# Hybrid attention and mixing layers: sums of products by twos in PSUM, word joins on GpSimd, shifted rows in PSUM, and a new order

## The chip, the cores and the metric

The kernel runs on one core of one Trainium2 chip. Its time is the device time of one execution in microseconds. Before the change three runs gave 1161.39, 1161.8 and 1164.65 us, median 1161.8. The engines are named as the profile names them: PE is TensorE (PEld its weight loads), DVE is VectorE, ACT is ScalarE, POOL is GpSimd, SP is SyncE, which here only issues DMAs.

## The reference

The input x has 8 sequences of 512 rows with 256 channels, all float32. Four layers follow each other; each takes the layer norm of x and adds its result to x:

```python
x = x + attn_a(layernorm(x))   # Q, K l2-normed; Q * mean over rows of K * V
x = x + ffn(layernorm(x))
x = x + attn_b(layernorm(x))   # 16 heads of 64, softmax over the queries
x = x + ffn(layernorm(x))      # the same weights as above

def ffn(x):                    # x_prev is x shifted down by one row, row 0 zero
    xr = mu_r * x + (1 - mu_r) * x_prev
    xk = mu_k * x + (1 - mu_k) * x_prev
    r = sigmoid(xr @ W_r.T)
    return r * (square(relu(xk @ W_k.T)) @ W_v.T)
```

In `attn_b` the projections q, k and v of one sequence are products of its 512 x 256 rows with 256 x 1024 weights, plus a bias each; the softmax runs over axis 2, the queries of the scores.

## The kernel before

The sequences b = 0 to 7 are worked on in halves h of 256 rows. A front of a sequence is `attn_a`, the first `ffn` and the norm of `attn_b`; then come 8 pairs of heads (g counts pairs over all sequences, 0 to 63); a tail is the second `ffn` with the write of the result.

**Attention.** `attend` (L1037) takes two pairs of heads at once: for each chunk c of 128 keys it issues the scores (`scores`, L959, four 64x512 matmuls into a pair of PSUM banks, a maximum on VectorE at L976), the context of the pair before (`context`, L1011) and the exponentials (`exps`, L981, ScalarE). `scale_v` (L995) divides the values by the sums: a reciprocal on VectorE (L1000) and a product on GpSimd (L1004), which the contexts wait for.

**Between two attention blocks** the other work is placed. Each piece is a Python generator, a chain, that yields before each step the engine, an assumed duration and when its input is ready; `Order` (L75) is a planner that runs in Python while the program is built. It keeps a clock for each engine, adds what a result takes to reach another engine (`PASS`, L33), and picks the chain whose next step can start first, with due times, and a rank that can be shifted by a pseudo-random number (`turn`, L171) seeded per block from the table `CHOICES`. What comes out is one fixed order of instructions; every engine works through its own part of it in order. PSUM is five slots for this: three pairs of banks, shared with the scores, and two single banks, shared with the contexts. A step on TensorE takes a slot (`take`, L107) and the chain gives it back (`give`, L128).

**Products.** For q, k and v of sequences 1 to 7, and of sequence 0 behind its first pairs and values, a 2 x 2 product of blocks is made with seven block products instead of eight (`seven`, L752), from sums of weights (`sums_of_weights`, L703, once) and of rows (`sums_of_rows`, L717, once for each sequence). A block product is `mul` (L813 for q and k, L848 for v): two 128x256 matmuls, each on its own half of a bank. There are 31 such chains for q and k (`project_pairs`, L803, two pairs of heads each) and 14 for v (`values_fast`, L841). The products are joined in SBUF: each goes into a bank of its own, which is read and given back, in the order 1, 6, 2, 7, 5, 4, 3. Product 1 is copied with its bias (`begin`: L823 on ScalarE for q and k, L860 on VectorE for v), products 6, 2, 4 and 3 are added by VectorE (L770, L774, L788, L792), product 7 with the difference of the biases (`join`: L831 for q and k; L867 and a GpSimd add at L870 for v), product 5 is copied by ScalarE (L780) and added twice by GpSimd (L783, L785).

**Norm and transposition.** `normed` (L349) takes mean and variance on VectorE (L355, L356), the sign change of the mean on VectorE (L372), the root and the shift on GpSimd (L374 to L376), and the scaling on ScalarE (L379); with `early` set the scaling is VectorE's (L365) and there is no shift. The transposed rows come either from TensorE (`normed_t`, L385, four 128x128 transposes for each half) or from a DMA transpose, which works on 16-bit words (`normed_dma`, L398): GpSimd splits the low and high words into two planes (L405, two copies), SyncE issues the transpose (L410), ScalarE joins the words (L414, one copy of 128x1024 words). The DMA way is taken for all norms of sequences 2 to 7 in the fronts and for the tails but the last.

**Mixing.** In `ffn` (L443) ScalarE writes the rows scaled by 1 - mu into two buffers, one row further on (L465), saves the last row of the first half (L462) as the edge of the second, VectorE fills the edge (L472) and adds mu times the rows (L479, two operations for each of xk and xr). Then TensorE makes k (L491), r and o (both in `rows`, L426), ScalarE takes the relu, the square and the tanh (L498, L501, L505), VectorE multiplies (L510) and `add_to` (L514) adds to x.

**Names.** Buffers come in two sets, with False and True in their names: xn, xp, xr, xk. The set True belongs to sequence 1's front and then to the tails of sequences 0 to 6. In the DMA way xr holds the split words, xk the transposed ones; xr (for mixing) or xp or xta (for products) holds the joined rows. `tr_*` are PSUM tiles of transposes, `m_qk` and `m_v` those of block products, sc scores, cx contexts.

## Time and profile before

| what | value |
|---|---|
| median of three runs | 1161.8 us (1161.39 to 1164.65) |
| the profiled execution, its own time | 1162.71 us |
| its span, from the first to the last instruction | 1160.8 us |
| mean granted clock of TensorE | 0.994 |
| instructions | 19186 |
| busy: PE, DVE, ACT, POOL | 97%, 69%, 63%, 42% of the span |
| DMA | 29.17 MB, mean 25 GB/s |

The profile is of one execution. A group row of it names line, engine, operation, the tiles written and read, partitions x elements and the count; behind the first bar stand the busy time in us and the mean ns of one instruction, behind the second the idle time of the engine just before them and what ended it. A row of the view of waits reads: engine, tile and line that waited, what it waited for, then the total in us, how many times, and the longest. A row of the timeline starts with the start and the length in us; in square brackets stands the idle time before it. In the view by windows each engine's busy time stands with its number of instructions, then the granted clock of TensorE, the DMA share and GB/s. Instructions of one engine overlap a little, so that a matmul's recorded length is longer than the distance to the next: two matmuls of 128x256 (four records) are 0.86 us apart from the next two.

### The profile page before, as it was taken

The numbers are of one execution on the slowest core, as the hardware profiler recorded it, in microseconds if no ns is written. First come the engines' busy times: TensorE is split into PE (matmuls) and PEld (weight loads), VectorE is DVE, ScalarE is ACT, GpSimd is POOL, SyncE is SP. The second block draws the span as 40 slices with busy tenths as digits, with TensorE's granted clock in tenths as the row PEclk, the third lists the DMA queues.
The fourth block names the chain that finished last, engine by engine and source line by source line (L and its number), as shares of the span: only waits on it lengthen the run. The fifth ranks groups of instructions, "written<-read, shape, count | busy, mean of one in ns | idle before, by whom it ended". The sixth has DMA issues, their size and how long they took to land.

```text
span 1160.8 us, 19186 instructions
## 1 busy us (share of the span) xinstructions
PE 1129.8 (97%) x7012; PEld 703.9 (61%) x7012; DVE 806.4 (69%) x1384; ACT 730.6 (63%) x1802; POOL 485.7 (42%) x702
## 2 busy tenths in 40 slices
PE   6999899999999999999999999999999999999997
PEld 3646466655668566656666655766657655666556
DVE  5676776777866767776886667676776777656853
ACT  3666575677855767657585568456774776556643
POOL 5465434443337334345532444442546343433211
PEclk9999899999999999999999999999999999999999
DMA  8000000110102100012000120001110100000001
GB/s 294 1 1 19 1 19 2 28 20 9 19 1 64 37 1 19 1 46 38 10 10 10 46 38 1 10 19 37 24 32 15 24 11 10 19 10 11 10 1 37
DMA packets 63294, 29.17 MB, mean 25 GB/s; under 512 B 53568, under 2 KB 61760, under 8 KB 62688
## 3 DMA queue, kind: packets, MB, share of 16 engines
q1 hardware_dynamic: 62048, 26.22, 9.4%
q8 instruction: 56, 0.92, 0.3%
q10 hardware_dynamic: 864, 1.05, 0.3%
q0 software_dynamic: 288, 0.67, 0.2%
q14 instruction: 38, 0.31, 0.1%
HBM read 10.63 MB, written 4.19 MB: 13 GB/s over the span
## 4 chain that ended last, share of the span: by engine, by line
PE 46%; DVE 2%; issue 1%; ACT 1%; DVEq 0%
PE cx L1024 10%; PE sc L971 10%; PE m_qk L815 8%; PE y L426 5%; PE m_v L850 4%; PE r_g L426 2%; PE o_g L426 2%; PE k_g L491 1%; PE r_f L426 1%; PE kv L571 1%; PE o_f L426 1%; PE k_f L491 1%; PE q L426 1%; DVE xrFalse L479 1%; DVE xrTrue L479 0%
## 5 line engine op out<-in xcount | busy, mean ns | idle before, releaser
L987 ACT ACTIVATE e<-sc,nm 128x512 f32<-128x512 f32 x512 | 346.6, 690 | 126.7 <-DVE nm L976 125.5
L976 DVE TENSOR_REDUCE nm<-sc 128x2 f32<-128x1024 f32 x256 | 307.9, 1216 | 60.9 <-PE sc L971 60.5
L971 PE MATMUL sc<-qk 64*64 64x512 f32 x2048 | 270.5, 600 | 9.4 <-DVE qk L792 8.3
L1024 PE MATMUL cx<-e,vs 64*64 64x512 f32 x2048 | 268.2, 594 | 0.2 <-POOL vs L1004 0.2
L1004 POOL TENSOR_TENSOR vs<-v,rs 128x256 f32<-128x256 f32 x128 | 78.5, 614 | 383.2 <-DVE rs L1000 363.3
L1024 PEld LDWEIGHTS cx<-e,vs 64*64 64x64 f32 x2048 | 85.4, 134 | 139.9 <-issue 115.9
L971 PEld LDWEIGHTS sc<-qk 64*64 64x64 f32 x2048 | 73.8, 133 | 151.4 <-issue 82.7
L426 PE MATMUL y<-al,ctx 128*128 128x256 f32 x512 | 116.3, 380 | 0.0
L426 PEld LDWEIGHTS y<-al,ctx 128*128 128x128 f32 x512 | 96.8, 190 | 17.3 <-ACT e L987 3.2
L987 ACT ACTIVATION_READ_ACCUMULATOR e<-sc,nm 128x1 f32 x512 | 105.6, 206 | 0.0
L1032 DVE TENSOR_TENSOR ctx<-cx,ctx 128x512 f32<-128x512 f32 x64 | 44.2, 691 | 48.0 <-ACT ctx L1031 46.9
L571 PE MATMUL kv<-wkv,xpFalse 128*128 128x512 f32 x112 | 52.4, 607 | 1.1 <-ACT xpFalse L414 1.1
L783 POOL TENSOR_TENSOR qk<-qk,qk 128x512 f32<-128x512 f32 x31 | 40.8, 1315 | 27.8 <-ACT qk L780 26.2
L913 DVE TENSOR_TENSOR x<-y,x 128x512 f32<-128x512 f32 x32 | 22.1, 689 | 39.9 <-PE y L426 39.7
L405 POOL COPY xrFalse<-xnFalse 128x512 uint16<-128x512 uint16 x72 | 42.6, 626 | 8.1 <-ACT xnFalse L379 8.1
L1031 ACT COPY ctx<-cx 128x512 f32<-128x512 f32 x64 | 37.5, 585 | 12.3 <-PE cx L1024 12.3
L517 POOL TENSOR_TENSOR x<-x,xkFalse 128x512 f32<-128x512 f32 x24 | 31.0, 1293 | 29.5 <-DVE xkFalse L510 21.9
L785 POOL TENSOR_TENSOR qk<-qk 128x512 f32<-128x512 f32 x31 | 40.6, 1310 | 2.4
L815 PE MATMUL m_qk<-xts,aq 128*128 128x256 f32 x124 | 37.1, 381 | 3.9 <-DVE v L788 3.9
L815 PE MATMUL m_qk<-xta,aq 128*128 128x256 f32 x124 | 38.2, 390 | 0.0
L770 DVE TENSOR_TENSOR qk<-m_qk,qk 128x512 f32<-128x512 f32 x31 | 21.4, 691 | 23.9 <-PE m_qk L815 23.3
L815 PE MATMUL m_qk<-xta,sums_q 128*128 128x256 f32 x124 | 36.9, 379 | 0.0
(248 smaller groups left out, 2037.5 us busy)
## 6 DMA issues: line engine op xcount, KB each, us to landing
out<-x SPq DMA_DIRECT2D x16, 256.0 KB, 2.1
x<-in_x SPq DMA_DIRECT2D x6, 512.0 KB, 4.3
aq<-in_aq SPq DMA_DIRECT2D x1, 1024.0 KB, 7.9
ak<-in_ak SPq DMA_DIRECT2D x1, 1024.0 KB, 9.9
av<-in_av SPq DMA_DIRECT2D x1, 1024.0 KB, 11.9
al<-in_al SPq DMA_DIRECT2D x1, 1024.0 KB, 14.3
xkFalse<-xrFalse SPq DMA_TRANSPOSE x36, 3.1
x<-in_x SPq DMA_DIRECT2D x4, 128.0 KB, 4.3
```

What stands on the lines that cost most here:

```text
L405: nc.gpsimd.tensor_copy(apart.rearrange("p (l k u d) -> p l k u d", l=2, k=KC, u=2)[:, :, :, u, :], s["xn"].bitcast(U16)[:, h, u, 2:].rear ...
L426: nc.tensor.matmul(ps[:, u * D : (u + 1) * D], lhsT=lhs[i][:, u * P : (u + 1) * P], rhs=rhs[i], start=(i == 0), stop=(i == n - 1),)
L571: nc.tensor.matmul(ps, lhsT=xt[:, kc, u * P : (u + 1) * P], rhs=wkv[:, kc, :], start=(kc == 0), stop=(kc == KC - 1),)
L783: nc.gpsimd.tensor_tensor(c12, c12, c22, ALU.add)
L815: nc.tensor.matmul(ps[:, w * HS : (w + 1) * HS], lhsT=lhs[w][n - 1], rhs=block_of_rows(b, n), start=True, stop=True,)
L850: nc.tensor.matmul(ps[:, u * HS : (u + 1) * HS], lhsT=block_of_rows(b, n)[:, u * P : (u + 1) * P], rhs=rhs[n - 1], start=True, stop=True,)
L971: nc.tensor.matmul(ps[m * HD : (m + 1) * HD, j, :], lhsT=kt[hs, keys], rhs=qt[hs, :], start=True, stop=True,)
L976: nc.vector.tensor_reduce(nm, ps, AX.X, ALU.max, negate=True)
L987: nc.scalar.activation(e[:, j, :], ps[:, j, :], AF.Exp, bias=nm[:, j : j + 1], accum_out=sums[g, h][:, c % 2, j : j + 1],)
L1004: nc.gpsimd.tensor_tensor(vs, vh[b, p // 4][:, 2 * h : 2 * h + 2, cols].rearrange("p t (j d) -> p t j d", j=2), rs.unsqueeze(3).to_broadca ...
L1024: nc.tensor.matmul(cx[m][j * HD : (j + 1) * HD, :], lhsT=vsc[g, c // 2][ks, c % 2, j, :], rhs=es[g, c][ks, j, :], start=(c == 0), stop=(c ...
L1032: nc.vector.tensor_tensor(ct, cx[1], ct, ALU.add)
```

## The change

The seven products are summed by twos in PSUM. Products 1, 6, 7 and 5 take a slot as before, but product 2 is accumulated on the bank of product 1 after that has been read, product 4 on that of 7, and product 3 on that of 5. So the banks of 1, 7 and 5 are held until their second reading, and product 5 is no longer copied and added by GpSimd. For v the difference of the biases is added by GpSimd to the summand before the join. The order of a chain is now 1, 6, 7, 2, 5, 4, 3.

The join of the words behind a DMA transpose moves from ScalarE to GpSimd, and so does the sign change of the mean from VectorE. In the mixing behind a DMA transpose (`mixed_dma`, new) ScalarE writes the shifted rows into a PSUM slot, one for xk and one for xr; VectorE clears the first column there, or fills it with the edge, and adds mu times the rows. The mixing behind TensorE's transposes (`mixed_t`) is what `ffn` did; the first mixings of sequences 0 and 1 take the `early` norm. The first norm of sequence 2 is transposed by TensorE. The planner gets marks that it lacked (the sums of weights, and the use of the buffers by the tail before), gates that open after an attention block, other assumed durations, a smaller allowance for other work inside a block, and a new `CHOICES` table, so that the whole order is a new one. The arithmetic and its types are the same otherwise.

The diff, cut to its core:

```diff
-PASS = {"T": 0.27, "A": 0.2, "V": 0.17, "G": 0.17, "S": 2.0}
+PASS = {"T": 0.27, "A": 0.2, "V": 0.17, "G": 0.17, "S": 2.2}
...
+        self.takes = step[5] if len(step) > 5 else self.on == "T"
...
-    def give(self):
-        self.banks = [self.ended if c is self.current else c for c in self.banks]
+    def give(self, i=None):
+        self.banks = [
+            self.ended if c is self.current and i in (None, n) else c
+            for n, c in enumerate(self.banks)
+        ]
     def ready(self, c):
         ready = max(c.ready, self.marks[c.mark])
-        if c.on == "T":
+        if c.takes:
             slots = self.slots(self.now)
             if slots:
                 ready = max(ready, slots[0][0])
...
         return [
             c for c in self.chains
-            if c.mark in self.marks and c.gate <= self.period
-            and (c.on != "T" or c.cost <= most and self.slots(self.now))
+            if c.mark in self.marks and c.gate <= self.open
+            and (c.on != "T" or c.cost <= most) and (not c.takes or self.slots(self.now))
         ]
...
         else:
             shift = small.tile([P, 2], F32, tag="shift", name=f"shift_{name}_{h}")
-            nc.vector.tensor_scalar(shift, mv[:, :, 0], -1.0, None, ALU.mult)
-            ready = yield "G", 1.3, ready
+            ready = yield "G", 1.4, ready
+            nc.gpsimd.tensor_scalar(shift, mv[:, :, 0], -1.0, None, ALU.mult)
             nc.gpsimd.tensor_scalar(rstd, mv[:, :, 1], LN_EPS, 1.0, ALU.add, ALU.mult)
             nc.gpsimd.tensor_tensor(rstd, rstd, neg_half[:, :2], ALU.pow)
             nc.gpsimd.tensor_tensor(shift, shift, rstd, ALU.mult)
...
-        ready = yield "G", 1.8, ready
+        ready = yield "G", 1.2, ready
...
         nc.sync.dma_start_transpose(
             out=turned.rearrange("p (g r) -> p g r", r=P), in_=apart
         )
-        ready = yield "A", 0.9, ready, -1, mark
-        nc.scalar.copy(
+        ready = yield "G", 1.25, ready, -1, mark
+        nc.gpsimd.tensor_copy(
             dst().rearrange("p k (s l) -> p l k s", l=2),
             turned.rearrange("p (l k s) -> p l k s", l=2, k=KC),
         )
...
-    edge = {}
-    def ffn(xb, name, s, h, ready, add_on, by_dma):
-        if by_dma:
-            ps = chunks(s["xr"], h)
-            ready = yield from normed_dma(
-                xb, name, s, h, ready,
-                lambda: s["xr"].bitcast(U16)[:, h, :].rearrange("p (k s) -> p k s", k=KC),
-            )
-        else:
-            ps, ready = yield from normed_t(xb, name, s, h, ready)
+    edge, begun = {}, set()
+    def mixed_t(xb, name, s, h, ready, xr, xk):
+        ps, ready = yield from normed_t(xb, name, s, h, ready, early=name in ("f0", "f1"))
         parts = ((1, s["xn"]), (0, s["xp"]))
-        if not edge:
+        if "fv" not in begun:
+            begun.add("fv")
             nc.gpsimd.tensor_scalar(fv, fv, 0.5, None, ALU.mult)
             order.place("G", 0.8, 0.0)
         ready = yield "A", 1.5, ready
...
-        xr, xk = chunks(s["xr"], h), chunks(s["xk"], h)
...
             if i == 1:
                 mixed = ready
-        if not by_dma:
+        order.give()
+        return mixed, ready
+    def mixed_dma(xb, name, s, h, ready, xr, xk):
+        ready = yield from normed_dma(
+            xb, name, s, h, ready,
+            lambda: s["xr"].bitcast(U16)[:, h, :].rearrange("p (k s) -> p k s", k=KC),
+        )
+        if h == 0:
+            ready = yield "A", 0.2, ready
+            edge[name] = small.tile([P, KC, 1], F32, tag="edge", name=f"edge_{name}")
+            nc.scalar.copy(edge[name], xr[:, :, HS - 1 :])
+        order.marks[name, h] = ready
+        for i, dst in ((1, xk), (0, xr)):
+            ready = yield "A", 0.8, ready, -1, None, True
+            ps = bank(f"prev_{name}_{h}_{i}").rearrange("p (k s) -> p k s", k=KC)
+            for kc in range(KC):
+                nc.scalar.activation(
+                    ps[:, kc, 1:], xr[:, kc, : HS - 1], AF.Identity, scale=omu[:, i, kc : kc + 1]
+                )
+            ready = yield "V", 0.93, ready, -1, (name, 0)
+            if h == 0:
+                nc.vector.memset(ps[:, :, 0:1], 0.0)
+            else:
+                nc.vector.tensor_tensor(
+                    ps[:, :, 0:1], edge[name], omu[:, i, :].unsqueeze(2), ALU.mult
+                )
+            for kc in range(KC):
+                nc.vector.scalar_tensor_tensor(
+                    dst[:, kc, :], xr[:, kc, :], mu[:, i, kc : kc + 1], ps[:, kc, :],
+                    ALU.mult, ALU.add,
+                )
+            if i == 1:
+                mixed = ready
             order.give()
+        return mixed, ready
+    def ffn(xb, name, s, h, ready, add_on, by_dma):
+        mix = mixed_dma if by_dma else mixed_t
+        xr, xk = chunks(s["xr"], h), chunks(s["xk"], h)
+        mixed, ready = yield from mix(xb, name, s, h, ready, xr, xk)
         done = yield "T", BANK, mixed
...
-        if b < 2:
-            ps, ready = yield from normed_t(xb, f"a{b}", s, h, ready, early=True)
+        if b < 3:
+            ps, ready = yield from normed_t(xb, f"a{b}", s, h, ready, early=b < 2)
             ready = yield "A", 0.5, ready
             nc.scalar.copy(xt, ps)
             order.give()
...
         (c11, c12), (c21, c22) = c
         def product(n):
             ready = yield "T", FAST, 0.0, -1, sums
-            ps = bank(f"m{n}_{name}")
-            mul(ps, n)
-            return ps.rearrange("p (u s) -> p u s", u=2), ready
-        ps, ready = yield from product(1)
-        u1 = yield from begin(ps, c11, ready)
-        order.give()
-        ps, ready = yield from product(6)
+            i = order.take()
+            ps = psum_tile(i, f"m{n}_{name}")
+            ps = ps[:, 0, :] if i < PAIRS else ps
+            mul(ps, n, True)
+            return i, ps, ps.rearrange("p (u s) -> p u s", u=2), ready
+        i1, b1, ps1, ready = yield from product(1)
+        u1 = yield from begin(ps1, c11, ready)
+        i6, _, ps6, ready = yield from product(6)
         u2 = yield "V", 0.62, max(ready, u1)
-        nc.vector.tensor_tensor(c12, ps, c11, ALU.add)
-        order.give()
-        ps, ready = yield from product(2)
-        yield "V", 0.62, max(ready, u1)
-        nc.vector.tensor_tensor(c11, ps, c11, ALU.add)
-        order.give()
-        ps, ready = yield from product(7)
-        u3 = yield from join(ps, c21, c12, max(ready, u2))
-        ps, p5 = yield from product(5)
-        p5 = yield "A", 0.5, p5
-        nc.scalar.copy(c22, ps)
-        order.give()
-        u6 = yield "G", 1.3, max(p5, u2)
-        nc.gpsimd.tensor_tensor(c12, c12, c22, ALU.add)
-        u7 = yield "G", 1.3, max(p5, u3)
-        nc.gpsimd.tensor_tensor(c22, c22, c21, ALU.add)
-        ps, ready = yield from product(4)
-        yield "V", 0.62, max(ready, u7)
-        nc.vector.tensor_tensor(c21, ps, c21, ALU.add)
-        order.give()
-        ps, ready = yield from product(3)
-        order.marks[name] = max(u7, (yield "V", 0.62, max(ready, u6)))
-        nc.vector.tensor_tensor(c12, ps, c12, ALU.add)
-        order.give()
+        nc.vector.tensor_tensor(c12, ps6, c11, ALU.add)
+        order.give(i6)
+        i7, b7, ps7, p7 = yield from product(7)
+        u3 = yield from join(ps7, c22, c12, max(p7, u2), True)
+        p2 = yield "T", FAST, u1, -1, None, False
+        mul(b1, 2, False)
+        yield from begin(ps1, c11, max(p2, u2))
+        order.give(i1)
+        i5, b5, ps5, p5 = yield from product(5)
+        c22_done = yield "V", 0.62, max(p5, u3)
+        nc.vector.tensor_tensor(c22, ps5, c22, ALU.add)
+        p4 = yield "T", FAST, u3, -1, None, False
+        mul(b7, 4, False)
+        yield from join(ps7, c21, c12, p4, False)
+        order.give(i7)
+        p3 = yield "T", FAST, c22_done, -1, None, False
+        mul(b5, 3, False)
+        order.marks[name] = yield "V", 0.62, p3
+        nc.vector.tensor_tensor(c12, ps5, c12, ALU.add)
+        order.give(i5)
...
+        for tag in ("sums_q", "sums_k"):
+            if tag not in order.marks:
+                yield "G", 0.0, 0.0, -1, tag
...
-        def mul(ps, n):
+        def mul(ps, n, start):
             for w in range(2):
                 nc.tensor.matmul(
                     ps[:, w * HS : (w + 1) * HS], lhsT=lhs[w][n - 1], rhs=block_of_rows(b, n),
-                    start=True, stop=True,
+                    start=start and w == 0, stop=True, skip_group_check=True,
                 )
...
-        def join(ps, dst, part, ready):
+        def join(ps, dst, part, ready, first):
             ready = yield "V", 0.79, ready
             for w in range(2):
                 nc.vector.scalar_tensor_tensor(
                     dst[:, w, :], ps[:, w, :], dbias[:, w, p // 2 : p // 2 + 1], part[:, w, :],
                     ALU.add, ALU.add,
                 )
-            order.give()
             return ready
...
         rhs = blocks_of_weights(av, blocks["sums_v"], split_values, half)
+        if "sums_v" not in order.marks:
+            yield "G", 0.0, 0.0, -1, "sums_v"
         yield "G", 0.0, 0.0, -1, ("vs", NP * (b - 1) + 3 + 4 * half, 1)
         v = vh[b, half] = one.tile([P, NT, 512], F32, tag=f"v{half}", name=f"v_{b}_{half}")
-        def mul(ps, n):
+        def mul(ps, n, start):
             for u in range(2):
                 nc.tensor.matmul(
                     ps[:, u * HS : (u + 1) * HS], lhsT=block_of_rows(b, n)[:, u * P : (u + 1) * P],
-                    rhs=rhs[n - 1], start=True, stop=True,
+                    rhs=rhs[n - 1], start=start and u == 0, stop=True, skip_group_check=True,
                 )
...
-        def join(ps, dst, part, ready):
+        def join(ps, dst, part, ready, first):
+            both = v[:, 0:2, 256:]
+            if first:
+                ready = yield "G", 1.3, ready
+                nc.gpsimd.tensor_tensor(both, part, spread(dvb[:, half, :]), ALU.add)
             ready = yield "V", 0.62, ready
-            nc.vector.tensor_tensor(dst, ps, part, ALU.add)
-            order.give()
-            ready = yield "G", 1.3, ready
-            nc.gpsimd.tensor_tensor(dst, dst, spread(dvb[:, half, :]), ALU.add)
+            nc.vector.tensor_tensor(dst, ps, both, ALU.add)
             return ready
...
-        yield from ffn(x[b], f"g{b}", buffers(not last), h, ready, add_on, not last)
+        if not last:
+            ready = yield "V", 0.0, ready, -1, ("g", b - 1, h) if b else ("n1", h)
+        order.marks["g", b, h] = yield from ffn(x[b], f"g{b}", buffers(not last), h, ready, add_on, not last)
...
             else:
                 order.fill(BANK)
             exps(g, c)
-            order.fill(0.0, 2.8)
+            order.fill(0.0, 1.0)
...
     total = B * (2.2 + 6 * BANK + 42 * FAST + 0.43 + 8 * BANK + 2 * FFN) - 4 * BANK - 2 * FFN
-    total -= 6 * 3.3 + 7 * 1.1
+    total -= 17 * 1.1 + 7 * 1.1
...
         order.place("T", CHANGE, 0.0)
+        order.open = g
...
```

## The prediction, made before the changed kernel ran

> **What bounds the kernel now.** The page's first and fourth parts come first: busy time by engine, and the chain that ended last.

> ```profile
> PE 1129.8 (97%) x7012; PEld 703.9 (61%) x7012; DVE 806.4 (69%) x1384; ACT 730.6 (63%) x1802; POOL 485.7 (42%) x702
> PE 46%; DVE 2%; issue 1%; ACT 1%; DVEq 0%
> ```

> TensorE is busy for 1129.8 of 1160.8 us, and no other engine reaches 70%. So work taken from ScalarE, VectorE or GpSimd is worth nothing by itself; it is worth what it takes off TensorE's waits. Those are the second view (who TensorE waited for: total, times, longest):

> ```profile
> PE sc L971 <- DVE qk L792: 8.3, 5, 3.4
> PE tr_a L393 <- DVE xnFalse L365: 6.4, 1, 6.4
> PE m_qk L815 <- DVE v L788: 3.9, 2, 2.0
> PE tr_f L393 <- ACT xnFalse L379: 2.1, 2, 1.9
> PE kv L571 <- ACT xpFalse L414: 1.1, 3, 0.7
> ```

> The 6.4 us are the first load and stay. With the waits too small for this fence, 15.4 us lie behind the first 60 us of the span, and 3.0 us lie in the opening behind the first load. The third view cuts the stages behind the two longest waits (3.43 us before 134.54, 2.50 us before 578.03); the column after the five engines is the granted clock:

> ```profile
> 134.50:141.20 6.70, 6.66 (x36) 2.10 (x40) 3.61 (x7) 1.45 (x4) 2.19 (x4) 0.54 0.01 2
> 141.30:148.00 6.70, 6.70 (x68) 2.36 (x64) 5.18 (x6) 5.46 (x16) 0.61 (x1) 1.00 0.00 0
> 578.00:581.60 3.60, 3.56 (x20) 1.19 (x24) 2.93 (x3) 0.25 (x1) 2.65 (x4) 0.59 0.02 5
> ```

> In equal time the slow stage holds 36 matmuls, the next 68. In the timeline four score and context groups take 134.54 to 141.04, 6.50 us, where four take 3.44 elsewhere (0.86 each): 3.06 us lost. Two groups from 578.03 to 581.24 lose 1.49. So the two waits cost 4.55 us more than their length. The next longest waits, 2.04 and 1.9 us, show a clock of 1.00 behind them. [...]

> Why VectorE is late shows in the fourth view, the timeline before one of the 2 us waits:

> ```profile
> 778.75 1.33 POOL L785 TENSOR_TENSOR v<-v 128x512 f32<-128x512 f32 x1
> 778.88 2.90 DVE L479 SCALAR_TENSOR_TENSOR xrFalse<-xrFalse,mu,xpFalse 128x256 f32<-128x256 f32 x2
> 782.98 0.69 DVE L788 TENSOR_TENSOR v<-m_v,v 128x512 f32<-128x512 f32 x1
> 783.72 0.70 PE L815 MATMUL m_qk<-xts,aq 128*128 128x256 f32 x2 [2.04 <-DVE v L788]
> ```

> Two mixing operations take 2.90 us beside GpSimd's adds; such a pair takes 0.88 us at 774.13. The add queued behind them starts at 782.98, TensorE 0.05 us after its end.

> **The change, part by part.** Rows used (mean ns behind the comma):

> ```profile
> L479 DVE SCALAR_TENSOR_TENSOR xrTrue<-xrTrue,mu,xpTrue 128x256 f32<-128x256 f32 x28 | 24.5, 916 | 0.0
> L831 DVE SCALAR_TENSOR_TENSOR qk<-m_qk,dbias,qk 128x256 f32<-128x256 f32 x62 | 27.1, 479 | 8.2 <-PE m_qk L815 8.0
> L414 ACT COPY xrTrue<-xkTrue 128x1024 uint16<-128x1024 uint16 x14 | 18.6, 1343 | 10.6 <-DMA xkTrue<-xrTrue 10.6
> L405 POOL COPY xrFalse<-xnFalse 128x512 uint16<-128x512 uint16 x72 | 42.6, 626 | 8.1 <-ACT xnFalse L379 8.1
> L783 POOL TENSOR_TENSOR qk<-qk,qk 128x512 f32<-128x512 f32 x31 | 40.8, 1315 | 27.8 <-ACT qk L780 26.2
> ```

> *Seven products.* TensorE still issues fourteen matmuls in each of the 45 chains (31 qk, 14 v). Accumulating ones cost what the others do: y, which accumulates four, has 380 ns, m_qk 379. GpSimd loses 90 adds of 1.31 us, 118 us; ScalarE loses 45 copies of 0.585 (26 us) and gains 62 of 0.478 (30 us); VectorE gains 0.18 us in each qk chain and 0.69 in each v chain, 15 us. The price is a wait: products 2, 4 and 3 now write where 1, 7 and 5 stand, so TensorE waits for their reader, and everything in TensorE's order stands behind it. A reader needs 0.16 us (a matmul's recorded end behind the next issue), up to 0.11 (VectorE's start), 0.69 and 0.05: 1.0 us behind the last issue of the product. I counted the matmuls between the two in the order of the changed program, at 0.86 us a product. For 2 behind 1 the least is 1.73 us, for 4 behind 7 also 1.73, where two operations need 1.2: covered. For 3 behind 5 it is 0.86 in 11 chains: 11 x 0.14 = **1.5 us**. From product 3 to the scores that read it the distance is 0.00 once (chain 6: VectorE's second join and last add end 1.04 us behind it) and 0.86 once (0.18 short), else at least 1.72: **1.2 us**. Before, chain 4 stands at 0.00 and waited 3.43 us, because its end also ran through GpSimd's adds. That cover needs a punctual VectorE.

> *Joins on GpSimd.* 48 word joins go from ScalarE (1.343 us, 65 us in all) to GpSimd's queue, where 128 scalings of v (614 ns) stand among them. Nothing shows a join there. From below: two splits of 512, L405, 1.25 us. From above: the one-input operation on 512 f32 at L457, 1.527 us, twice, 3.05. I take 1.25, the same type and nearly the same pattern: 60 us. With 56 sign changes moved from VectorE (60 of 0.31 us) at 0.2, GpSimd's total is 486 - 118 + 60 + 11 = 439 us, less than now. A join that waits for its transpose now holds a scaling, not an exponential; I cost that at nothing, because contexts waited 0.2 us for scalings in the whole run. [...]

> *Mixing in PSUM.* ScalarE writes the shifted, scaled rows (104 activations, as before; 0.50 us from SBUF, 0.48 from PSUM, so no change either way) into PSUM. VectorE's 104 operations then read one operand there. Now they average 0.77 us; with a PSUM operand L831 shows 0.479 and the `tr` forms of L479 0.474, never the 1.5 us extremes. That takes 30 us off VectorE and, more to the point, the 2 us delays. The edge clears add 26 small operations, 0.10 to 0.36 us each (rows of 128x2), some 4 us. VectorE's clear or edge waits for ScalarE, with chain adds queued behind it, as L472 did. Each mixing half holds one of five PSUM slots twice, and each chain two instead of one; new slot waits lie between nothing and the 3.9 us which slot waits (L815 behind L788) cost now.

> *Front 2 by TensorE.* Eight transposes, 0.87 us by the timeline (122.73 to 123.60), and two DMA transposes fewer in SyncE's queue. **+0.9 us.**

> *New order and marks.* Other work inside the 32 attention blocks falls from 11 blocks to 5 on VectorE, with ScalarE nearly free of it in both. Between blocks I summed VectorE's instructions by their rows: the fullest stage was 17.2 us beside 20.3 us of matmuls, and is 13.2 beside 17.7. In the opening the 2.1 us wait for `tr_f` goes: one kv and one q product more stand ahead of it. But `v` now follows the transpose of n0 at once, and its copy (0.17 + 0.6 + 0.1) is 0.9 late; with 0.2 at that transpose the opening gains 3.0 - 0.8 - 1.1 = 1.1. The end keeps its distances: 3.45 us from each of the last k to its o, both times.

> *Sum*, against the profiled execution (span 1160.8, 1162.7 with 1.9 around it): the 13.0 us of waits for VectorE behind the opening (8.3 + 3.9 + 0.8 small) go, with 4.55 us of slow clock and 1.1 in the opening; 2.4 us of other waits stay; added are 0.9 + 1.5 + 1.2. 1160.8 - 18.65 + 3.6 = 1145.8, and 1147.7 with what lies around. The median of the runs is 0.9 below the profiled one: **1147 us**.

> **Rivals.**
> 1. *Half the gain* (15%). Joins at 3.05 us make kv and mixing late. Against it: GpSimd stays below half busy. Price: 36 joins feed kv or mixing; if a tenth of the 36 x 1.8 us arrives, 6.5 us: 1154.
> 2. *Slower* (17%). One mechanism: VectorE's clear or edge waits for ScalarE, that for the join, that for the transpose, and the chain's add behind it now holds TensorE itself. Transposes land in 3.0 to 6.2 us, median 3.1 (the source view of L410), and ScalarE now sits 42 us idle for them. For it: 26 mixing halves, chains with 0.14 us less than nothing to spare. Against it: the same chain stood before and its waits for ScalarE were small. It decides at 15 / 26 = 0.57 us of TensorE a half; at 1.0 the time is 1173, more if waits of 2.5 us bring the slow clock.
> 3. *Nothing gained* (8%). The waits only move: 135 accumulating products at 0.1 us are 13.5 us, 1160. Against it: only 11 are counted short.

> **How the numbers follow.** Forecast 60%, rivals 15, 17 and 8. The low end takes all waits but the first load away: 1160.8 - 15.4 - 4.55 - 3.0 + 0.9 + 1.9 - 0.9 = 1139.8; some must stay, so 1141. The high end reaches past rivals 1 and 3, 1161. About 0.3% (3.5 us) is what a measurement of this kernel can tell from none: faster 0.75, same 0.08, slower 0.17.

> **What would show it.** Right: mixing operations near 0.48 us in every form; score waits for VectorE below 3 us in total; a granted clock of 1.00 but for the ends; joins near 1.25 us; a TensorE busy time some 4 us lower. Wrong: many waits of m_qk or m_v for VectorE's adds; waits of kv or contexts for GpSimd; a clock below 1 in mid-span; VectorE idle for ScalarE ahead of a clear.

## The result and the profile after

The changed kernel takes 1153.5 us (median of four runs, 1151.3 to 1154.2) beside 1161.6 for the kernel before on the same chip: ratio 0.9922, 95% interval 0.9906 to 0.9938. It is faster, by 8 us where 14.6 were forecast. The profiled execution took 1151.3 us, the fastest of the four, with a span of 1149.6; the other three took 1153.2 to 1154.2 us at a mean granted clock of 0.996 to 0.999, where the profiled one shows 1.000.

The first part of the page after (busy time by engine), and the chain that ended last:

```profile
PE 1127.1 (98%) x7020; PEld 702.6 (61%) x7020; DVE 780.2 (68%) x1403; ACT 671.8 (58%) x1763; POOL 440.3 (38%) x708
PE 75%; DVE 1%; DMA 0%; issue 0%; ACT 0%; POOL 0%; POOLq 0%; DVEq 0%
```

TensorE bounds the kernel as before, its idle time falls from 31.0 to 22.5 us, and the chain now runs through TensorE alone for three quarters of the span (46% before). GpSimd is 1.3 us above the total worked out ahead (439), ScalarE some 2 us above what the terms of the prediction give (730.6 - 65 - 26 + 30). Next, who TensorE waited for (total, times, longest), after:

```profile
PE tr_a L399 <- DVE xnFalse L371: 6.9, 1, 6.9
PE cx L1072 <- POOL vs L1052: 4.0, 2, 3.4
PE cx L1072 <- DVE v L832: 1.0, 1, 1.0
PE sc L1019 <- DVE qk L832: 0.9, 1, 0.9
...
PE m_qk L858 <- DVE qk L814: 0.7, 1, 0.7
```

The 8.3 us that scores and the 3.9 us that products waited for VectorE's sums are gone but for 0.9 and 1.0 us (0.7 shown). In their place stand contexts: for GpSimd's scalings of v 4.0 us, which was 0.2 us before, and for VectorE's last sum of v 1.0 us. The rows of the mixing and of the joins, after (total us, mean ns of one, idle before them):

```profile
L514 DVE SCALAR_TENSOR_TENSOR xrTrue<-xrTrue,mu,prev_g 128x256 f32<-128x256 f32 x28 | 12.2, 477 | 0.5
...
L420 POOL COPY xrTrue<-xkTrue 128x1024 uint16<-128x1024 uint16 x14 | 18.8, 1340 | 24.2 <-DMA xkTrue<-xrTrue 24.2
L420 POOL COPY xrFalse<-xkFalse 128x1024 uint16<-128x1024 uint16 x12 | 16.0, 1337 | 27.8 <-DMA xkFalse<-xrFalse 27.8
```

The mixing is 477 or 478 ns in all four forms. A join is 1.34 us, what it was on ScalarE, but GpSimd's queue now stands 79 us idle behind transposes (last column: 24.2 + 27.8 here, 27 in the other two forms).

**Where the new wait comes from.** The timeline of the changed kernel between 634 and 647 us, of SyncE's queue, of VectorE's reciprocal, of GpSimd, and of the matmul that ended the wait (start, length, engine and line; in brackets the idle time before it and what ended that):

```profile
634.71 1.25 SPq L416 DMA_TRANSPOSE xkFalse<-xrFalse  x1
637.06 0.38 SPq L976 DMA_DIRECT2D out<-x  x1
639.27 0.38 SPq L271 DMA_DIRECT2D x<-in_x  x1
639.75 1.25 SPq L416 DMA_TRANSPOSE xkFalse<-xrFalse  x1
...
640.07 0.17 DVE L1048 RECIPROCAL rs<-sums 128x4 f32<-128x4 f32 x1
...
644.62 1.33 POOL L420 COPY xrFalse<-xkFalse 128x1024 uint16<-128x1024 uint16 x1 [5.38 <-DMA xkFalse<-xrFalse]
645.88 1.19 POOL L1052 TENSOR_TENSOR vs<-v,rs 128x256 f32<-128x256 f32 x2
...
646.55 1.09 PE L1072 MATMUL cx<-e,vs 64*64 64x512 f32 x8 [3.39 <-POOL vs L1052]
```

Read from below: TensorE waited 3.39 us for the first of two scalings. The reciprocal that it needs was there at 640.24, but GpSimd could not make it sooner because a join stood ahead of it, 5.38 us idle for its transpose. The transpose was issued at 639.75, though its words were split by 635.80: SyncE's queue had a store ahead of it, which itself waited for its rows until 637.03, and then a load into the buffer of that store, issued 2.2 us behind the store, when that had landed. Besides, this transpose landed 4.8 us after its issue, the longest of all 48 (median 3.1). The same sequence (store 770.94, load 773.23, transpose 773.77) gives the other 0.65 us. It stands a third time at 494.17 to 496.80, where the join was idle for 7.47 us and no context waited: what a stall costs depends on what stands behind it.

### The profile page after: what moved, and what is told of

The parts are those of the page before. It is cut to its first block, busy times and chain, and to the rows that moved or that the text cites. A ratio compares the mean times of both kernels' runs of the same rounds, so it can differ in the third digit from the quotient of the medians.

```text
span 1149.6 us, 19062 instructions
## 1 busy us (share of the span) xinstructions
PE 1127.1 (98%) x7020; PEld 702.6 (61%) x7020; DVE 780.2 (68%) x1403; ACT 671.8 (58%) x1763; POOL 440.3 (38%) x708
## 4 chain that ended last, share of the span: by engine, by line
PE 75%; DVE 1%; DMA 0%; issue 0%; ACT 0%; POOL 0%; POOLq 0%; DVEq 0%
PE cx L1072 16%; PE sc L1019 15%; PE m_qk L858 13%; PE y L432 8%; PE m_v L894 6%; PE kv L613 3%; PE o_g L432 2%; PE r_g L432 2%; PE k_g L533 2%; PE k_f L533 2%; PE r_f L432 2%; PE o_f L432 2%; PE q L432 2%; DVE nm L1024 1%; DMA xkFalse<-xrFalse 0%
## 5 line engine op out<-in xcount | busy, mean ns | idle before, releaser
L1072 PE MATMUL cx<-e,vs 64*64 64x512 f32 x2048 | 265.2, 590 | 5.1 <-POOL vs L1052 4.0
L1019 PE MATMUL sc<-qk 64*64 64x512 f32 x2048 | 266.8, 593 | 1.0 <-DVE qk L832 0.9
L866 ACT ACTIVATE qk<-m_qk,bias 128x256 f32<-128x256 f32 x124 | 52.2, 476 | 56.9 <-PE m_qk L858 53.5
L874 DVE SCALAR_TENSOR_TENSOR qk<-m_qk,dbias,qk 128x256 f32<-128x256 f32 x124 | 54.0, 477 | 18.3 <-PE m_qk L858 17.3
L619 ACT COPY av<-kv 128x256 f32<-128x256 f32 x32 | 11.9, 373 | 54.8 <-PE kv L613 52.2
L411 POOL COPY xrFalse<-xnFalse 128x512 uint16<-128x512 uint16 x68 | 39.6, 616 | 8.5 <-ACT xnFalse L385 8.5
```

Source lines behind the costliest of these rows:

```text
L866: nc.scalar.activation(dst[:, w, :], ps[:, w, :], AF.Identity, bias=bias[:, w, p : p + 1])
L874: nc.vector.scalar_tensor_tensor(dst[:, w, :], ps[:, w, :], dbias[:, w, p // 2 : p // 2 + 1], part[:, w, :], ALU.add, ALU.add,)
L1019: nc.tensor.matmul(ps[m * HD : (m + 1) * HD, j, :], lhsT=kt[hs, keys], rhs=qt[hs, :], start=True, stop=True,)
L1072: nc.tensor.matmul(cx[m][j * HD : (j + 1) * HD, :], lhsT=vsc[g, c // 2][ks, c % 2, j, :], rhs=es[g, c][ks, j, :], start=(c == 0), stop=(c ...
```

## The experiments

**Theory.** The time is TensorE's work and its waits. The gain is VectorE's punctuality (sums without GpSimd's adds, mixing without the stretch), and some 6 us of it are given back because joins now hold scalings when a transpose is late in SyncE's queue. **Rivals.** The new order alone made the gain; or the joins' move off ScalarE did; or GpSimd is simply too full. Four runs (store and load behind the next transpose, joins on ScalarE, shifted rows in SBUF, both undone) stood on one chip, with a median of 1162.3 for the kernel before; the other runs on two more, with 1161.4 and 1161.2. "Load later" in the names below means that SyncE's queue order is changed as in the run that follows first.

### Store and load behind the next transpose

The second half's store and load are put into a list, and issued right behind the next transpose; all other engines keep their order, and nothing is left out.

```
+    held = []
         nc.sync.dma_start_transpose(...)
+        while held:
+            held.pop(0)()
...
-        nc.sync.dma_start(out=rows_out[:, ts, :], in_=x[b][:, ts, :])
-        if both(f"g{b}") and b + 4 < B:
-            load_x(b + 4)
+        if both(f"g{b}") and b + 4 < B:
+            held.extend([leave, lambda: load_x(b + 4)])
```

> The changed kernel with only SyncE's queue changed: where a second half of a finished batch is stored and its buffer loaded again, the store and the load are issued behind the next DMA transpose instead of ahead of it; all other engines keep their instructions in order. Theory (the transpose at 639.75 was ready at 635.8 but queued behind a store and a load that waits 2.2 us for that store; its join then held the scaling): the context waits for GpSimd of 3.4 and 0.6 us fall below 0.5 in total; TensorE's waits 17.6 to about 13.5 us; time 1149 to 1150.5, 3 to 4.5 us below the changed kernel. Rival (the join is late for another reason, GpSimd being full or the transpose itself being slow): the waits stay at 3 us or more and the time stays within 1 us.

Measured: 1147.1 us (1146.4 to 1148.1), ratio to the kernel before 0.9875, interval 0.986 to 0.989. The same stretch, SyncE's queue and then GpSimd; below it the busy times and TensorE's three longest waits:

```profile
634.42 2.66 SPq L425 DMA_TRANSPOSE xkFalse<-xrFalse  x2
637.18 0.56 SPq L989 DMA_DIRECT2D out<-x  x1
639.70 0.38 SPq L280 DMA_DIRECT2D x<-in_x  x1
...
637.89 2.67 POOL L431 COPY xrFalse<-xkFalse 128x1024 uint16<-128x1024 uint16 x2 [1.15 <-DMA xkFalse<-xrFalse]
640.48 0.62 POOL L1069 TENSOR_TENSOR vs<-v,rs 128x256 f32<-128x256 f32 x1
```

```profile
PE 1126.5 (98%) x7020; PEld 703.0 (61%) x7020; DVE 779.9 (68%) x1403; ACT 671.7 (59%) x1763; POOL 440.5 (38%) x708
...
PE tr_a L408 <- DVE xnFalse L380: 6.7, 1, 6.7
PE cx L1089 <- DVE v L843: 1.0, 1, 1.0
PE sc L1036 <- DVE qk L843: 0.9, 1, 0.9
```

Both transposes leave together, both joins run from 637.89 on, and the scaling stands at 640.48, 5.4 us sooner. No context waits for GpSimd in the whole run, TensorE's idle time is 18.1 us (1144.6 - 1126.5). The theory holds, and the rival of a full GpSimd falls: its busy time is the same to 0.2 us. The rival of a slow transpose falls as a cause of its own, but the late transpose was also slow: the two that were issued right behind a load landed after 4.8 and 4.6 us, and land after 3.3 and 3.1 here. So the new place in the queue takes away the late issue and the slower transfer together. The gain is above the expected 3 to 4.5: 5.5 us by the two ratios, 6.4 by the medians. The profiled executions are 5.0 us apart in span, 4.0 of it the two waits. This kernel's four runs show a mean clock of 0.999 to 1.000; that the changed kernel's three longer ones (0.996 to 0.999) paid for a slow clock behind the wait at 646 fits, but their timelines weren't recorded. This version beats both kernels.

### Joins on ScalarE again

```
-        nc.gpsimd.tensor_copy(
+        nc.scalar.copy(
             dst().rearrange("p k (s l) -> p l k s", l=2),
```

> The changed kernel with one part undone: the 48 joins of the transposed words are copied by ScalarE again; matmuls and VectorE's instructions keep their order. Theory (the gain is VectorE's punctuality, and part of it is given back because a join that waits for its transpose now holds scalings behind it on GpSimd): the context waits for the scaling vs of 3.4 us at 646 and 0.6 us at 780 go, no score is late for VectorE, and what comes in their place is a join that holds exponentials on ScalarE, some tenths each; GpSimd's busy time falls by 64 us to about 376, ScalarE's rises by 64 to about 736; time 1149.5 to 1152, 2 to 4 us below the changed kernel. Rival (the gain is the new order of the work alone, not the engines that do it): within 1 us of the changed kernel. Second rival (moving the joins off ScalarE is where the gain came from): 1156 or more, with contexts waiting for exponentials.

Measured: 1172.5 us (1170.8 to 1172.9), ratio 1.009 (1.0077 to 1.0104). The theory was wrong by 20 us on this run, and the second rival's number came out, though it is scores that wait and not contexts:

```profile
PE sc L1019 <- ACT e L1035: 11.1, 8, 4.9
PE tr_a L399 <- DVE xnFalse L371: 6.7, 1, 6.7
```

Scores now wait for exponentials, up to 4.9 us, with a clock of 0.57 over the 7 us behind the longest, and TensorE's busy time is 12.1 us longer (1139.2). The joins' old place isn't free: in the changed order they stand ahead of exponentials that TensorE soon needs.

The same with load later, to see how much of it is the late transposes:

> The run with joins on ScalarE, and besides the store and load issued behind the next transpose. Theory: of the 19 us that joins on ScalarE cost in this order, the part that comes from transposes queued behind a store and a load goes: the score waits for exponentials at 646 (4.9 us) and 786 (2.1 us), and the slow clock behind the first (0.91 over 40 us, 3.6 us); the waits at 500 to 560, 950 and 960 stay, since there a join on ScalarE holds exponentials for a transpose that nothing delays: 1160 to 1164. Rival (ScalarE has too much work with 48 joins, wherever they stand): within 3 us of the run with joins on ScalarE, 1169 or more.

Measured: 1159.9 us (1158.6 to 1160.3; kernel before 1161.4 on this chip), ratio 0.9985 (0.9973 to 0.9996), just below the expected 1160 to 1164. So 12.6 of the 19 us were late transposes, which cost twice as much ahead of exponentials as ahead of scalings (6.4). The rival (too much work on ScalarE wherever it stands) fails by its number, 1169 or more, but as much again, 12.7 us against load later (1147.1), does not come from late transposes: score waits of 3.6 us in seven places, and 8.2 us of TensorE's busy time (1134.7 against 1126.5). Why the busy time is longer was not followed up; short waits inside the records would fit.

### Shifted rows in SBUF again

```
-            ps = bank(f"prev_{name}_{h}_{i}").rearrange("p (k s) -> p k s", k=KC)
+            order.take()
+            ps = s["xn" if i else "xp"][:, h]
```

> The changed kernel with one part undone: the shifted and scaled rows of the mixing lie in SBUF buffers of the set, where they lay before, instead of a PSUM bank; the PSUM bank is still set aside by the planner, so that matmuls, VectorE and GpSimd keep their order. Theory (the mixing operations with two SBUF operands are stretched beside GpSimd, and the stretch makes sums late that scores and products wait for): the mean of the 104 mixing operations goes from 0.48 back to about 0.81 us with single ones of 1.5, VectorE's busy time rises by 30 to 35 us to about 812, score and product waits for VectorE go from 1.9 us back to 6 to 10 us, with a stage of slow clock behind one of over 2.5 us; time 1158 to 1163. Rival (new order alone): 1153.5 within 1 us, since the order is the same; the stretched operations fall into VectorE's idle time.

Measured: 1157.2 us (1156.0 to 1158.5), ratio 0.9961 (0.9948 to 0.9975): 3.6 us above the changed kernel by the medians, 4.5 by the ratios, just below the expected 1158 to 1163, and not the rival's "within 1". The rows with the largest and the smallest mean of its four forms, and its busy times:

```profile
L515 DVE SCALAR_TENSOR_TENSOR xrTrue<-xrTrue,mu,xpTrue 128x256 f32<-128x256 f32 x28 | 23.3, 870 | 1.5
...
L515 DVE SCALAR_TENSOR_TENSOR xkFalse<-xrFalse,mu,xnFalse 128x256 f32<-128x256 f32 x24 | 12.1, 545 | 1.7 <-DVE xnFalse L509 0.4 <-ACT xnFalse L504 0.3 <-ACT xpFalse L504 0.2
...
PE 1130.4 (98%) x7020; PEld 703.0 (61%) x7020; DVE 797.8 (69%) x1403; ACT 666.5 (58%) x1763; POOL 444.8 (39%) x708
```

The stretch is back (single ones up to 1.5 us), but the mean over all is 0.65, not 0.81 (23.3 + 16.9 + 15.2 + 12.1 over 104); that with GpSimd's 90 adds gone there is less beside which to stretch fits. TensorE waits for VectorE's sums in three new places, 1.0 us in all. The longest wait is still the one for the scalings, 3.8 us here, and now a slow clock follows it (mean 0.66 over 5 us; the changed kernel shows 1.00 there). With load later that wait is out of the way:

> The run with the shifted rows in SBUF, and besides the store and load issued behind the next transpose: what the mixing in PSUM is worth when no wait of over 3 us stands in the middle. Theory: the mixing in SBUF makes sums late a little in several places (1.9 us of waits for VectorE and ScalarE in all, none near the length that slows the clock): 1148.5 to 1151, so 1.5 to 4 us above the changed kernel with that queue order, less than the 3.6 us between the two with the old queue order, where the wait of 3.8 us at 646 brought a slow clock with it (0.91 over 20 us). Rival (the price of the stretch doesn't depend on that wait): 3.6 us or more above, 1150.7 or more.

Measured: 1151.1 us (1150.5 to 1151.1), ratio 0.9913 (0.99 to 0.9927), 4.0 us above load later by the medians, 4.4 by the ratios. Here the rival is right: the price doesn't depend on that wait. In the profile 1.6 us of it are idle time (1149.3 - 1129.6 against 18.1) and 3.1 are busy time at a full clock: kv records of 609 instead of 599 ns, sc and cx 0.9 and 1.2 us more in total. That these 3.1 us are small delays spread over many stages is our reading; no view shows them one by one. The mixing in PSUM is worth about 4 us in this order.

### Both undone

The two edits above in one kernel.

> The changed kernel with both parts undone: joins on ScalarE and shifted rows in SBUF, as in the kernel before; what is left of the change is the sum of products in PSUM by twos, the new marks and the new order. Theory: like the run with the shifted rows in SBUF alone, but without the context waits for scalings: 1155 to 1161, so at most 6 us of the gain of 8.1 stay. Rival (order alone, or the sum in PSUM alone): 1153.5 or less, the whole gain stays. What the two single runs cost should add up to this one within 2 us; if not, the two parts hide each other's waits.

Measured: 1173.4 us (1172.3 to 1174.3), ratio 1.010 (1.0086 to 1.0114). Beside joins on ScalarE alone (1172.5) the mixing costs 0.9 us; the two don't add up (19 + 3.6); that scores which wait for exponentials give VectorE time to be late in would explain it, and isn't shown. The theory's 1155 to 1161 was wrong with the joins. The rival falls too: what is left, the sums in PSUM, the marks and the order, is 11 us slower than the kernel before, so they don't carry the gain without the other two parts.

### The kernel before with load later

> The kernel before, with only SyncE's queue changed: the store and the load wait until the next transpose is issued, or until the loaded rows are asked for; two of the four pairs move. Theory (in the kernel before, the late transposes held exponentials by a join on ScalarE for up to 4.45 us and TensorE still had work, so their price was hidden): within 1.5 us of the kernel before. Rival (the queue cost the kernel before as much as it costs the changed one): 1155 to 1158, and then the changed kernel's gain over it would be no more than what the other parts bring.

Measured: 1161.8 us (1160.6 to 1164.4, kernel before 1161.4), ratio 1.0007 (0.9996 to 1.0017). The number is the theory's, its reason is not. In the kernel before, the joins of the two transposes that move (issued at 508.97 and 788.33) had no idle time before them, so nothing waited for these transposes; and the join that stood idle for 4.45 us waited for a transpose with no load ahead of it, which landed in the usual 3.1 us. The price in SyncE's queue is new with the changed order, though the queue is not. As in the changed kernel, the two transposes right behind a load landed late: after 6.2 and 4.8 us, and after 3.1 us, both, in this run.

### The old sums within the changed order

With load later; product 5 is copied out by ScalarE and added twice by GpSimd, products 2, 4 and 3 start afresh. The edit in part:

```
-        mul(b1, 2, False)
+        mul(b1, 2, True)
...
-        nc.vector.tensor_tensor(c22, ps5, c22, ALU.add)
+        nc.scalar.copy(c22, ps5)
+        nc.gpsimd.tensor_tensor(c12, c12, c22, ALU.add)
+        nc.gpsimd.tensor_tensor(c22, c22, c21, ALU.add)
```

> The changed kernel with the store and load behind the next transpose, and the sums of the seven products made as in the kernel before, within the changed order: products 2, 4 and 3 start afresh in the bank they had, product 5 is copied out by ScalarE and added twice by GpSimd (90 adds more, and the added values' bias 28 times as before), VectorE makes the other sums with a second operand in SBUF. Theory (GpSimd's adds make sums late, and stretch what VectorE does beside them): against the run with that queue order (1147.1), GpSimd's busy time rises by 90 to 110 us to about 540, product and score waits for VectorE and context waits for GpSimd come back with 8 to 20 us: 1155 to 1170. Rival (the sums were never what TensorE waited for; the order did it): 1147 to 1150.

Measured: 1241.4 us (1236.8 to 1242.1), ratio 1.068 (1.0659 to 1.0702). Who VectorE waited for:

```profile
DVE qk L818 <- POOL qk L845: 83.1, 30, 4.9
...
DVE v L818 <- POOL v L845: 38.4, 13, 4.8
```

43 times VectorE stands idle for GpSimd's adds, 2.8 us on average, 121.5 us in all; in the kernel before those were 15.3 + 2.8 us. The direction is the theory's; the time is 71 us beyond its 1155 to 1170, and isn't a price of the old sums: as these waits show, the changed order leaves the last products no room for those adds, and the order of the kernel before did. The run shows that the new sums and the new order need each other, and not what either is worth.

### Other orders

The changed kernel with the table of the kernel before, then both kernels with one neutral entry `CHOICES = ((0, 0, 0),)`.

> The changed kernel with the table of choices of the kernel before, so that the planner puts the work in another order. Theory (the gain is the engines' punctuality, and the table only picks where the leftovers fall): 1150 to 1159, faster than the kernel before; waits for VectorE below 6 us, and its own waits where a join or a sum is late. Rival (the gain is the table): 1160 or more.

Measured: 1245.5 us (1243.3 to 1250.8), ratio 1.0732 (1.0711 to 1.0753). By the number that is the rival's side, and the theory is wrong in that the parts don't make the engines punctual in every order. The next pair shows that this table is 22 us worse for the changed kernel than none: a table fits the kernel that it was made for, and the run doesn't tell where the gain of 8 us comes from.

> The changed kernel with its table of 34 choices replaced by one neutral entry, so that the planner decides alone. With the other kernel's table it took 1245, so the order matters more than any part. Theory (the parts make the engines punctual whatever the order): faster than the kernel before with the neutral table, by 5 us or more. Rival (the gain of 8 us stands on the chosen order alone): as slow as the kernel before with the neutral table, or slower by any amount.

> The kernel before with its table of choices replaced by the same neutral entry; the partner of the changed kernel without its table. Theory: 1170 to 1230, and 5 us or more above the changed kernel without its table. Rival: equal to it or below.

Measured: changed kernel 1223.5 us (1222.0 to 1224.5), ratio to the kernel before with its table 1.0537 (1.052 to 1.0555); the kernel before without its table 1229.7 (1225.7 to 1231.1), ratio 1.0582 (1.0562 to 1.0603). The changed one is 6 us faster without either table, which speaks for the parts and against the order alone, but one pair of orders 70 us off the chosen ones is weak proof. What the two waited for says more; first the changed kernel, then the kernel before, both neutral:

```profile
PE cx L1065 <- DVE xrTrue L507: 11.5, 3, 5.4
PE cx L1065 <- POOL vs L1045: 8.6, 4, 4.2
PE cx L1065 <- DVE xnFalse L618: 7.9, 5, 2.8
PE sc L1012 <- DVE qk L825: 7.8, 8, 1.6
```

```profile
PE sc L964 <- DVE qk L785: 34.7, 12, 5.2
PE cx L1017 <- ACT xnTrue L491: 6.7, 2, 3.9
```

Scores waiting for VectorE's sums fall from 34.7 to 7.8 us: the sums come in time in another order too, though the two neutral orders are not the same one, so that the parts alone do this isn't shown. But contexts now wait for the scalings behind joins (8.6) and for the mixing (11.5 on `xrTrue` alone). A context doesn't read `xrTrue`; by the code it needs both single banks of PSUM (`context` clears them), and shifted rows can hold those until VectorE has mixed them. One of these waits, in the timeline of the changed kernel with the neutral table:

```profile
739.44 0.87 DVE L507 SCALAR_TENSOR_TENSOR xrTrue<-xrTrue,mu,prev_g 128x256 f32<-128x256 f32 x2
...
740.46 1.13 PE L1065 MATMUL cx<-e,vs 64*64 64x512 f32 x4 [5.44 <-DVE xrTrue L507]
```

So both new prices are real, and the chosen order avoids the second wholly (no such wait after) and the first but for 4.0 us.

## Why the prediction was right, and where it was wrong

The forecast was a span of 1145.8 us; the profiled one is 1149.6, 3.8 longer. The median of the runs, forecast as 1147, is 1153.5; the other 3 us are there because the profiled execution is the fastest after, where before it was 0.9 above the median. By its terms:

| term of the sum | forecast, us | measured in the profile, us |
|---|---|---|
| waits for VectorE's sums behind the opening (13.0) | -13.0 | -11.0 (0.7 + 0.3 + 1.0 stay) |
| slow clock behind two of them | -4.55 | -4.55 |
| opening | -1.1 | +1.3 (first load 6.9 for 6.4, the rest 3.8 for 3.0) |
| other waits | 0 | -2.2 (kv 1.1, exponentials 0.6, issue 0.5) |
| eight transposes | +0.9 | in TensorE's busy time, not told apart; taken as 0.9 |
| product 3 behind 5 | +1.5 | +2.2 |
| scores behind product 3 | +1.2 | +0.9 |
| joins holding scalings | 0 | +3.8 |

The column adds up to -8.65 where the span fell by 11.2. The other 2.55 us aren't explained; about half of them lie in gaps too small to be listed (TensorE's idle time fell by 8.5, the waits above by 7.2), and half in TensorE's busy time (fell by 2.7; slow clock, transposes and product 3 give 1.45).

- **What bounds it: right.** 130 us less busy time on VectorE, ScalarE and GpSimd (26.2, 58.8 and 45.4) came to 8 to 11 us of time, all of it TensorE's.
- **Why VectorE is late: right, and shown.** The mixing measures 0.477 in PSUM and 0.65 in SBUF in the same order, and the second costs 4 us. The same stretch is still there where both operands of a VectorE operation lie in SBUF: four of L685 take 3.69 us beside GpSimd's add, twice what four at their median of 478 ns take, and TensorE's `m_qk` waited 0.67 us for the sum behind them (L814). VectorE and GpSimd in the changed kernel:

```profile
903.09 3.69 DVE L685 SCALAR_TENSOR_TENSOR xkFalse<-xkFalse,rnq,gf 128x256 f32<-128x256 f32 x4
...
903.25 1.44 POOL L913 TENSOR_TENSOR v<-v,dvb 128x512 f32<-128x512 f32 x1 [0.80 <-DVE v L814]
...
906.70 0.68 DVE L814 TENSOR_TENSOR qk<-m_qk,qk 128x512 f32<-128x512 f32 x1
```

  The prediction took the stretch out of the mixing and forgot that L685 has it too: that, with the `m_qk` (0.3) and the context (1.0) that wait within the next 10 us, while VectorE works without a gap, is the 2.0 us that stay of the 13.0.
- **Joins at 1.25 us: right in size (1.34), wrong in what they hold.** The step that failed is "A join that waits for its transpose now holds a scaling, not an exponential; I cost that at nothing, because contexts waited 0.2 us for scalings in the whole run." Those 0.2 us were measured while no join stood in that queue, so they said how punctual VectorE's reciprocals were and nothing of what a stalled join would do. That joins stand idle was in the profile before (42 us, single ones of up to 4.45), and so was a late transpose behind a store and a load, though no join waited for one there; the prediction did not follow either into the new order. Put ahead of the scalings, a stall of 5.38 us was worth 3.39. The run with the store and load behind the transpose takes it away and measures 1147.1, the time that was forecast. That it meets the forecast so closely is luck: 2.4 us more in the opening and 2.0 us of sums that stayed are offset by 2.2 us of other waits that went and the 2.55 that aren't explained.
- **Product 3 behind product 5: right.** It shows as longer records, not as waits: in 10 chains (11 were counted) the first matmul of product 3 starts 0.30 to 0.40 us behind the one before it instead of 0.22, and the next 0.32 behind it, 2.2 us in all. Its group, `xta,sums_q`, which holds products 3 and 5, went from 379 to 389 ns; 10 of the 62 records of product 3 have 483 ns, none had before.
- **Scores behind product 3: right.** One wait of 0.9 us, at 160 to 180 us, the chain with distance 0.00.
- **Opening: wrong.** The wait for `tr_f` went, but `v` waits for its copy (0.7) and for VectorE (0.7), kv twice (0.8 and 0.6), `o_f` 0.4: 3.8 us where 1.9 were forecast. Of these the copy, the first kv and 0.2 at a transpose were counted; `v` behind VectorE, the second kv, `o_f` and `tr_f` (0.4) were not. No run here was made on it.
- **Slow clock: right in the profiled execution.** It shows a clock of 1.00 up to the last microseconds. That is in part luck: the wait of 3.39 us fell across two windows of the clock (2.00 and 1.39 us of them without a matmul, last section), and the three other runs, at 0.996 to 0.999, paid for some slow clock.
- **VectorE's clears behind ScalarE (rival 2): not in this order.** VectorE stood 1.6 us idle for ScalarE ahead of a clear or an edge in the whole run. With the neutral table contexts wait up to 5.4 us for the mixing: there is a price in another order, but by the PSUM slot and not by VectorE's queue as the rival had it.
- **Half the gain (rival 1): the size came true by luck.** It wanted joins of 3 us that make kv and mixing late; the joins are 1.34 us, and what was late were scalings.

Whether the sums in PSUM or the order they allowed brought the 11 us of span isn't settled. With the neutral table score waits for sums fall from 34.7 to 7.8 us, in two orders that differ, which speaks for the parts; with the changed table each part undone costs from 4 to 94 us, and the table was made for all of them.

## What to carry to other kernels

A join that waited for its DMA cost here what stood behind it in its queue (3.39 us of TensorE where that was a scaling, after 5.38 us idle; nothing where no context waited, after 7.47), so when such an instruction moves to another engine, its possible stalls must be laid over the new queue, and followed back to the queue that issues the transfer. A store followed by a load into the same buffer held that queue here until the store had landed (2.2 us); issue what is urgent ahead of the pair. Where an order was chosen for one assignment of work, undoing a part of it measures the misfit as well as the part.

## What the runs showed of the hardware

```profile
641.74:645.16 3.42, 1.42 (x16) 1.00 0.72 201
645.16:648.57 3.41, 2.02 (x20) 1.00 0.00 0
648.57:651.98 3.41, 3.41 (x33) 1.00 0.00 0
```

```profile
641.74:645.15 3.41, 2.67 (x28) 1.00 0.80 196
645.15:648.57 3.42, 0.34 (x4) 1.00 0.14 31
648.57:651.98 3.41, 3.41 (x20) 0.50 0.00 0
```

  The first wait leaves 2.00 and 1.39 us of two windows idle and the clock stays; the second leaves 3.08 us of one, and the next window holds 20 matmuls for 33. A window at half speed costs 1.7 us, an estimate from its 3.41 us. The kernel before shows it in its times: three of 34 executions on two chips took 1157.9 to 1158.0 us at a mean clock of 0.999, the others 1160.3 to 1164.7 at 0.994 to 0.997.
- **GpSimd copied 1024 16-bit words a partition as fast as ScalarE:** 1.34 us on both (L414 before, L420 after), each word written two words on from the one before it.
- **The mixing was stretched only with both operands in SBUF and a GpSimd operation beside:** 104 mixing operations never exceed 0.48 us with one operand in PSUM, 56 of them beside a GpSimd instruction. With both in SBUF in the same order, the 54 that had no GpSimd instruction beside them took 0.47 to 0.49 us, the 50 that had one 0.47 to 1.51. Why isn't shown here.
